# A macaron layer with two levels of seven-product matmuls: sums of weights kept in DRAM, and a down projection that accumulates in PSUM

## The chip, the core and the metric

The kernel runs on one core of a Trainium2 chip. The metric is the device time of one execution in microseconds (us); the figure for the kernel before is the median of three runs. A profile is one execution of the same program with the hardware profiler on. Engines are named as the profile names them: PE is TensorE (PEld its weight loads), DVE is VectorE, ACT is ScalarE, POOL is GpSimd, SP is SyncE, whose queue issues all DMAs here.

## What is computed

A layer of 2048 tokens by 512 features in float32: half of an MLP, then causal attention with 16 heads of 32, then half of the same MLP again. All three work on a layer norm of `x` and add to `x`.

```python
x = x + 0.5 * ffn(layernorm(x), gate, up, down)      # 4-bit codes and scales, 4096 rows
x = x + attn(layernorm(x), w_qkv, b_qkv, w_out, b_out)
x = x + 0.5 * ffn(layernorm(x), gate, up, down)      # the same weights

def ffn(x, Wg, Wu, Wd):                              # the weights are dequantized first
    g, u = x @ Wg.T, x @ Wu.T                        # 512 -> 4096
    return (gelu_tanh(g) * u) @ Wd.T                 # 4096 -> 512
```

## The kernel before

**Seven products for eight.** Each big matmul is split into 2 by 2 blocks and done as seven block products in place of eight (Winograd's form of Strassen's scheme). It needs sums of blocks of the weights (`s3 = a11 - a21`, `s2 = a22 - s3`, `a21 + a22`, `s4 = a12 - s2`), like sums of the tokens (`t3`, `t2`, `t1`, `t4`), and sums of the seven results.

**First MLP** (`ffn`, lines 186 to 570; its phase 2 isn't used). The 4096 rows are eight groups `g` of 512, each with two halves `h`. The codes are dequantized on DVE (`dequant_steps`, L217), the outer sums of the weights are made on POOL (`Rows.steps`, L263), and dequantized weights with their sums are written to DRAM (`keep`, L244) for the second MLP: 14 blocks of 128 by 256 for each `(g, h)`, and 14 for the down weights of each `g`. The order is written out by hand. `slot` (L320) does the seven gate and seven up products of one half for half of the tokens. After every product it runs `pump(rate)` (L309), which takes `rate` steps from the list `background` (the dequantizing and summing of coming weights, 20 steps for a half of a group, 16 for the down weights), and, in two of the four slots of a group, one token or down step of `sums` and one piece of the down projection (`down_pieces`, L386). At the end of a slot what is left in `background` is run at once. Codes are loaded when `Rows.load` or `down_steps` is called, that is before the steps that use them, in the SP queue.

**Attention** (`attention`, L1008) follows. In its pairs of heads 5 and 6 (L1383) it starts what the second MLP needs first: `load_first` fetches the weights of two pairs of problems, `sums_first` forms their inner sums. At its end (L1434 to L1444) come the last value products, eight pieces of the output projection, the last four divisions (reciprocals on DVE, L1253; multiplications on POOL, L1256) and four last pieces of the projection.

**Second MLP** (`second_ffn`, L599). Here the seven-product scheme is used twice, one level inside the other, and the tokens are done in two halves of 1024. An outer product `i` of `(g, h)` is called a problem; `problems` (L573) lists the 112 of one half of the tokens, seven to each `(g, h)`, in the order 1, 2, 6, 7, 5, 4, 3, and two neighbours form a pair: NP = 56 pairs for a half, numbered `n` = 0 to 111 through both. Seven pairs are one group `g`. In what follows "place" is `n % 7`.

- `fetch` (L583) loads a pair's weights into one of four ring slots, four pairs ahead. One DMA for each of the two problems brings the 4 blocks; `weight_sums` (L591) forms the inner sums in place, four POOL instructions for a pair, two pairs ahead of use.
- `pair` (L681) runs the seven inner products `y`. Each is four PE matmuls of 128x128 on 128x256. Products 1, 6, 7 and 4 add up in one PSUM bank `d`, 5 and 3 in a bank `f`, 2 has a bank `e`. The partial sums are read between them: after 1, 5 and 6 by ACT copies (L721, L726, L734), after 2, 7 and 3 by DVE additions (L730, L737, L740), after 4 by ACT (L743). So PE may issue 6 only after ACT has read 1, 7 after ACT has read 6, and 4 after DVE has read 7 (L737). Between them lie other products and, at "a" and "b" of the order (1, 5, 2, 6, a, 7, 3, b, 4), pieces of the down projection. Without pieces the order is (1, 5, 6, 2, 7, 3, 4). `hooks` are steps that are issued after the product of that count.
- `recombine` (L750) adds the results of the pair before (L758: of the 14 additions in a group, 10 on DVE and 4 on POOL, 1024 elements each), then gelu on ACT (L761) and the gating product on DVE (L770). The additions are issued at hook 1, gelus at hook 4, gating at hook 6.
- `down` (L800) does the down projection of a group during the seven pairs of the next group. `down_sums` are four DVE additions of 1024 elements (L809 to L812), all issued at place 1. Its 14 pieces (seven products for each of two quarters `q`) are run two to a pair. A piece is eight PE matmuls (L823) into a bank of its own, which DVE (L832) or ACT (L846) reads; sums of the seven results are made in SBUF by six DVE instructions, two ACT copies and five POOL additions (L838) for each `q`.
- `Tokens.outer` and `Tokens.inner` (L643, L658) form the sums of the tokens, on DVE but for one. They are issued at hooks of the first pairs of each half (L927 to L959); `Later` (L878) normalizes and transposes the second half of the tokens about pairs 53 to 56.
- PSUM has a pool `ps_one` of seven banks and `ps_acc` of one, which the second MLP before leaves unused.

Of the kernel before, what the change touches and what calls it, by code (L numbers as in the profile page):

```python
# [35 lines left out]
def macaron_kernel(ctx: ExitStack, tc: tile.TileContext, x, packed, scales, wqk, bqk, wv, bv, wo, bo, out):  # L36
# [147 lines left out]
    kept = {}  # L184

    def ffn(phase, finish, behind, loads, ready=(), first_w=None):
# [8 lines left out]
        with tc.tile_pool(name=f"w{phase}", bufs=1) as wp, tc.tile_pool(name=f"dq{phase}", bufs=1) as dq, tc.tile_pool(  # L195
# [52 lines left out]
            class Rows:  # L248
# [28 lines left out]
                def keep(self):  # L277
                    keep((self.g, self.h), self.flat)

# [243 lines left out]
            for g in range(NG):  # L523
# [13 lines left out]
                if phase == 1:  # L537
                    background += down_steps(wd, g)
                    second.keep()
                else:  # L540
                    nc.sync.dma_start(out=wd, in_=kept[g])
# [14 lines left out]
                if phase == 1:  # L556
                    keep(g, wd)
# [25 lines left out]
    def fetch(slot, pair):  # L583
        for k, (g, h, i) in enumerate(pair):
            place = {1: 0, 5: 1, 2: 2, 4: 3, 7: 4, 6: 5, 3: 6}[i]
            nc.sync.dma_start(
                out=slot[:, k, 0:4, :].rearrange("p (m c) n -> p m (c n)", m=2),
                in_=kept[g, h].rearrange("p (m i c n) -> p i m (c n)", m=2, i=7, c=2)[:, place],
            )

    def weight_sums(slot):  # L591
        a11, a12, a21, a22, s3, s2, s4 = [slot[:, :, y, :] for y in range(7)]
        eng = nc.gpsimd
        eng.tensor_tensor(s3, a11, a21, ALU.subtract)
        eng.tensor_tensor(s2, a22, s3, ALU.subtract)
        eng.tensor_tensor(a21, a21, a22, ALU.add)
        eng.tensor_tensor(s4, a12, s2, ALU.subtract)

    def second_ffn(finish, ready, slots):  # L599
# [9 lines left out]
        with tc.tile_pool(name="w2", bufs=1) as wp, tc.tile_pool(name="act2", bufs=1) as ap:  # L609
# [20 lines left out]
            class Tokens:  # L630


                def __init__(self, half, b1, b2):
                    nm = f"f2_{half}"
                    self.b1, self.b2 = b1, b2
                    self.ts, self.t4 = x_transposed(nm, 2), x_transposed(nm, 3)
                    self.ys = wp.tile([P, 7, 3, 256], F32, tag="ys", name=f"ys_{nm}")
# [5 lines left out]
                def outer(self, first):  # L643
                    b11, b21, b12, b22, t3, t2, t4 = [self.operand(x) for x in range(7)]
                    return [
                        lambda: first.tensor_tensor(t3, b22, b12, ALU.subtract),
                        lambda: tt(t2, t3, b11, ALU.add),
                        lambda: tt(b12, b12, b11, ALU.subtract),
                        lambda: tt(t4, b21, t2, ALU.subtract),
                    ]  # L650

                def first_sum(self, x):

                    if x < 2:
                        return self.t4[:, 2, 256 * x : 256 * x + 256]
                    return self.operand(x)[:, 0, 256:]

                def inner(self, t):  # L658
# [6 lines left out]
                    t1 = b12 if t > 0 else self.t4[:, 2, :].rearrange("p (x n) -> p x n", x=2)  # L665
                    return [
                        lambda: tt(t3, b22, b12, ALU.subtract),
                        lambda: tt(t1, b12, b11, ALU.subtract),  # L668
# [4 lines left out]
                def factors(self, i):  # L673
                    x = (None, 0, 1, 3, 6, 2, 5, 4)[i]
                    v = self.operand(x)
                    t3, t2, t4 = [self.ys[:, x, k, :] for k in range(3)]
                    return [None, v[:, 0, :256], v[:, 1, :256], v[:, 1, 256:], t4, self.first_sum(x), t2, t3]
# [3 lines left out]
            def pair(n, tokens, pieces, hooks):  # L681
# [3 lines left out]
                fa = [[None] + [a[:, k, y, :] for y in (0, 1, 6, 3, 2, 5, 4)] for k in range(2)]  # L685
# [16 lines left out]
                def product(ps, y, first=False):  # L702

                    for k in range(2):
# [3 lines left out]
                        )  # L708

# [89 lines left out]

            def down(half, g):  # L800


                def block(h, second):
# [5 lines left out]
                    lambda: tt(s3, block(0, 0), block(0, 1), ALU.subtract),  # L809
                    lambda: tt(block(0, 1), block(0, 1), block(1, 1), ALU.add),  # L810
                    lambda: tt(s2, block(0, 1), block(0, 0), ALU.subtract),
                    lambda: tt(s4, block(1, 0), s2, ALU.subtract),  # L812
                ]
                u = {}
                x_half = residual[:]

# [740 lines left out]
```

## Time and profile before

| what | value |
|---|---|
| median of three runs | 3265.59 us (3264.62 to 3267.82) |
| the profiled execution, its own time | 3266.22 us |
| its span, first to last instruction | 3264.4 us |
| granted PE clock, mean | 0.992 |
| PE, PEld, DVE, ACT, POOL busy in the span | 97%, 61%, 67%, 32%, 52% |
| first MLP, 0 to 1194 us: PE, DVE, POOL busy | 1178, 761, 616 us |
| attention, 1194 to 2107.57 us: PE, DVE, POOL busy | 901, 536, 233 us |
| second MLP, 2107.57 to 3264.4 us: PE, DVE, POOL busy | 1096, 904, 851 us |

A row of the view of stages has a window in us from the span's start, its length, the busy time of each engine in it with its number of instructions, the granted PE clock, the share of the DMA engines' time and GB/s. Matmuls overlap in the record: one of 128x256 is shown with 0.38 us, but four of them start 0.86 us after the four before (2306.87, 2307.73, 2308.59 us in the timeline), so that a busy PE isn't yet a PE at its pace. In the view of waits a line has who waited for whom, the total in us, how often, and the longest.

### The profile page before, as it was taken

How to read it: one execution, taken by the hardware profiler on the slowest of the kernel's cores; microseconds unless marked ns; L12 is line 12 of the kernel's file. 1: busy time of each engine (PE TensorE's matmuls, PEld its weight loads, DVE VectorE, ACT ScalarE, POOL GpSimd, SP SyncE). 2: the span in 40 equal slices, each digit the busy share in tenths (PEclk: the TensorE clock that was granted, in tenths of full speed). 3: DMA queues.
4: the chain of work that ended last, by engine and by line, in shares of the span. 5: the costliest groups of instructions: out<-in, count | busy, mean ns of one | idle time of the engine just before them, and what ended most of it. 6: DMA issues, size and time to landing. Idle time of an engine off the chain costs nothing.

```text
span 3264.4 us, 39140 instructions
## 1 busy us (share of the span) xinstructions
PE 3175.8 (97%) x14000; PEld 1987.7 (61%) x14000; DVE 2201.7 (67%) x3078; ACT 1044.7 (32%) x2134; POOL 1700.0 (52%) x1785
## 2 busy tenths in 40 slices
PE   8999999999999999999999999899999999999998
PEld 4556565655656565333344333378888878888887
DVE  6666666666666555575654665578778887777786
ACT  4111111111111131464543545433333333333332
POOL 3546364555546340332212233367778767777775
PEclk9999999999999999999999999999999999999999
DMA  4111111111111100000000000122222233222221
GB/s 142 65 71 42 65 71 49 65 65 71 42 65 65 52 17 7 6 15 6 13 4 6 21 19 8 67 90 84 78 81 84 75 104 126 75 75 84 78 81 56
DMA packets 118562, 186.91 MB, mean 57 GB/s; under 512 B 11176, under 2 KB 89000, under 8 KB 114400
## 3 DMA queue, kind: packets, MB, share of 16 engines
q1 hardware_dynamic: 118368, 184.41, 17.2%
q8 instruction: 111, 1.82, 0.2%
q14 instruction: 83, 0.68, 0.1%
HBM read 132.24 MB, written 50.56 MB: 56 GB/s over the span
## 4 chain that ended last, share of the span: by engine, by line
PE 84%; DVE 9%; issue 3%; ACT 2%; POOL 2%; DMA 0%; SPq 0%; DVEq 0%; POOLq 0%; ACTq 0%
PE po L414 12%; PE pu L315 11%; PE pg L315 11%; PE d_f L705 9%; PE po_f L823 9%; PE av L1217 8%; PE pm L1152 6%; PE f_f L705 4%; PE pqk L1063 4%; PE ps L1278 2%; PE e_f L705 2%; PE pv L1080 2%; PE pp L1102 1%; PE ps L1287 1%; DVE o_f L758 1%
## 5 line engine op out<-in xcount | busy, mean ns | idle before, releaser
L1167 DVE TENSOR_REDUCE parts<-pm 128x1 f32<-128x512 f32 (+3 forms) x640 | 370.5, 607 | 151.2 <-PE pm L1152 138.2
L705 PE MATMUL d_f<-ys_f,ring 128*128 128x256 f32 x1344 | 353.2, 386 | 48.8 <-DVE o_f L737 47.8
L1152 PE MATMUL pm<-kT,qT 32*128 32x512 f32 (+3 forms) x1280 | 335.6, 576 | 0.1
L1310 ACT ACTIVATE pt<-ps 128x512 f32<-128x512 f32 (+3 forms) x576 | 271.7, 532 | 131.7 <-PE ps L1287 130.8
L705 PEld LDWEIGHTS d_f<-ys_f,ring 128*128 128x128 f32 x1344 | 254.6, 192 | 95.8 <-DVE o_f L737 57.7
L1217 PE MATMUL av<-pt,vaug 128*64 128x512 f32 (+3 forms) x1280 | 301.2, 555 | 7.9 <-ACT both L1226 7.2
L1287 PE MATMUL ps<-qT,kT 32*128 32x512 f32 (+3 forms) x1280 | 279.0, 536 | 0.0
L758 DVE TENSOR_TENSOR o_f<-o_f,o_f 128x1024 f32<-128x1024 f32 x128 | 251.4, 1974 | 34.7 <-ACT o_f L743 32.5
L369 POOL TENSOR_TENSOR u<-u,u 128x512 f32<-128x512 f32 x64 | 81.9, 1279 | 345.2 <-ACT u L366 345.2
L1304 POOL TENSOR_SCALAR_AFFINE_SELECT pt<-pt 128x256 f32<-128x256 f32 x128 | 52.3, 408 | 396.4 <-ACT pt L1303 396.1
L823 PE MATMUL po_f<-wd_f,inter_f 128*128 128x256 f32 x1024 | 241.2, 379 | 1.6 <-DVE inter_f L770 1.6
L414 PEld LDWEIGHTS po<-wd,inter 128*128 128x128 f32 x1024 | 194.4, 190 | 77.5 <-issue 55.7
L414 PE MATMUL po<-wd,inter 128*128 128x256 f32 x1024 | 241.1, 379 | 0.0
L315 PE MATMUL pg<-xT_f,w 128*128 128x512 f32 x512 | 240.8, 598 | 0.0
L705 PE MATMUL f_f<-xT_f,ring 128*128 128x256 f32 x896 | 237.1, 388 | 3.6 <-DVE xT_f L668 3.6
L315 PE MATMUL pu<-xT_f,w 128*128 128x512 f32 x512 | 238.0, 592 | 0.0
L428 POOL TENSOR_TENSOR xq<-xq,d 128x512 f32<-128x512 f32 x124 | 160.3, 1303 | 114.3 <-DVE d L422 63.5
L823 PEld LDWEIGHTS po_f<-wd_f,inter_f 128*128 128x128 f32 x1024 | 194.4, 190 | 28.3 <-DVE inter_f L770 2.0
L705 PEld LDWEIGHTS f_f<-xT_f,ring 128*128 128x128 f32 x896 | 175.2, 196 | 29.6 <-DVE xT_f L668 2.5
L1217 PEld LDWEIGHTS av<-pt,vaug 128*64 128x64 f32 x1280 | 65.3, 135 | 209.3 <-issue 147.4
L823 PE MATMUL po_f<-wd_f,s_f 128*128 128x256 f32 x768 | 181.0, 379 | 1.3 <-issue 1.3
L414 PE MATMUL po<-wd,s 128*128 128x256 f32 x768 | 181.4, 379 | 0.0
(193 smaller groups left out, 6125.2 us busy)
## 6 DMA issues: line engine op xcount, KB each, us to landing
wd_f<-kept SPq DMA_DIRECT2D x112, 256.0 KB
kept<-wd SPq DMA_DIRECT2D x8, 1792.0 KB
xq<-in_x SPq DMA_DIRECT2D x16, 256.0 KB
pk<-in_gate_codes SPq DMA_DIRECT2D x16, 256.0 KB
sc<-in_gate_scales SPq DMA_DIRECT2D x32, 128.0 KB
pk<-in_up_codes SPq DMA_DIRECT2D x16, 256.0 KB
sc<-in_up_scales SPq DMA_DIRECT2D x32, 128.0 KB
pk<-in_down_codes SPq DMA_DIRECT2D x16, 256.0 KB
```

The lines of the kernel that those rows point to most:

```text
L315: nc.tensor.matmul(ps, lhsT=a[:, j, :], rhs=b[:, j, :], start=(j == 0), stop=(j == 1))
L414: nc.tensor.matmul(ps[:, j, :], lhsT=a[i][:, k, bass.ts(2 * q + j, P)], rhs=b[i][:, k, :], start=(k == 0), stop=(k == 1),)
L428: adder.tensor_tensor(dst, dst, other, ALU.add)
L705: nc.tensor.matmul(ps[:, k, :], lhsT=fa[k][y], rhs=fb[k][y], start=first and k == 0, stop=True, skip_group_check=True,)
L758: sums.append(lambda: eng.tensor_tensor(dst, dst, other, ALU.add))
L823: nc.tensor.matmul(ps[:, j, :], lhsT=a[:, k, bass.ts(2 * q + j, P)], rhs=wd[:, PLACE[i], k, :], start=(k == 0), stop=(k == 1),)
L1063: nc.tensor.matmul(ps, lhsT=w[:, j, k, :], rhs=xT[tb][:, k, :], start=(k == 0), stop=(k == 3))
L1152: nc.tensor.matmul(ps[a][:, :n], lhsT=q[r, bass.ts(4 * g + i, P)], rhs=k[r, kb * 512 : kb * 512 + n], start=True, stop=not on_pe,)
L1167: nc.vector.tensor_reduce(parts[:, a, i, kb : kb + 1], ps[a][:, :n], AX.X, ALU.max)
L1217: nc.tensor.matmul(av[64 * a : 64 * a + 64, off:], lhsT=vaug[:, c, p % 4, HD * a : HD * a + 2 * HD], rhs=pt[:, a, off:], start=(c == 0), s ...
L1287: nc.tensor.matmul(ps[a][:, off:], lhsT=k[r, bass.ts(c, P)], rhs=q[r, g * 512 + off : (g + 1) * 512], start=False, stop=True,)
L1310: nc.scalar.activation(pt[:, a, plain:], ps[a][:, plain:], AF.Exp, scale=scale)
```

## The change

Three things in the second MLP change, and the first MLP does more.

- **Inner sums of the weights.** The first MLP makes the four inner sums of all seven blocks (`inner_sums`) on POOL, in two parts of four and three blocks, into tiles of the tag `xn` (two buffers), and writes each part to DRAM (`kept_sums`): eight POOL instructions and eight DMAs for each `(g, h)`. They are steps of `background`. `fetch` now brings seven blocks in three DMAs for a problem, and `weight_sums` is gone.
- **Down projection.** Products 1, 6, 7 and 4 of a quarter add up in one bank (`ps_acc`; for the last quarter of all `ps_one`), 5 and 3 in another, 2 in a third, as the inner products do. ACT reads after 1, 6 and 5, DVE after 2, 7, 4 and 3: four DVE, three ACT and three POOL instructions for each `q`. The order is (1, 2, 6, 7, 4, 5, 3), named `DOWN`, for the first quarter and (1, 2, 6, 7, 5, 4, 3) for the second. The four `down_sums` are issued at places 1 (two), 2 and 3, and 1, 1, 2, 2, 2, 2 and 4 pieces at places 0 to 6. In the second half of the tokens pair 56 takes one piece and runs one after it, pair 57 takes none.
- **Sums of the tokens.** Those that the second MLP needs first are made at the end of attention on DVE (`outer_sums`, `inner_first`), ahead of the last value products and the last divisions. For the second half of the tokens two of the four outer sums go to POOL.

```diff
+                def inner_sums(self):
+                    key = self.g, self.h
+                    kept_sums[key] = store.tile([P, 4, 7, P], F32, tag=f"kept_sums_{key}", name=f"kept_sums_{key}")
+                    steps = []
+                    for part in (slice(0, 4), slice(4, 7)):
+                        a11, a12, a21, a22 = [self.w[:, m, part, c, :] for m in range(2) for c in range(2)]
+                        made = []
+                        def make(k, x, y, op, part=part, made=made):
+                            t = normed(f"inner_{phase}_{self.g}_{self.h}_{k}_{part.start}")
+                            t = t[:, : (part.stop - part.start) * P].rearrange("p (i n) -> p i n", n=P)
+                            made.append(t)
+                            nc.gpsimd.tensor_tensor(t, x, made[k - 1] if y is None else y, op)
+                            nc.sync.dma_start(out=kept_sums[key][:, k, part, :], in_=t)
+                        steps += [
+                            lambda f=make, x=a11, y=a21: f(0, x, y, ALU.subtract),
+                            lambda f=make, x=a22: f(1, x, None, ALU.subtract),
+                            lambda f=make, x=a12: f(2, x, None, ALU.subtract),
+                            lambda f=make, x=a21, y=a22: f(3, x, y, ALU.add),
+                        ]
+                    return steps
...
-                    background += down_steps(wd, g)
+                    background += down_steps(wd, g) + rows.inner_sums()
...
+                    background += second.inner_sums()
                     keep(g, wd)
...
-            nc.sync.dma_start(
-                out=slot[:, k, 0:4, :].rearrange("p (m c) n -> p m (c n)", m=2),
-                in_=kept[g, h].rearrange("p (m i c n) -> p i m (c n)", m=2, i=7, c=2)[:, place],
-            )
+            w = kept[g, h].rearrange("p (m i c n) -> p i m c n", m=2, i=7, c=2)[:, place]
+            nc.sync.dma_start(out=slot[:, k, 0:2, :], in_=w[:, 0])
+            nc.sync.dma_start(out=slot[:, k, 2, :], in_=w[:, 1, 1])
+            nc.sync.dma_start(out=slot[:, k, 3:7, :], in_=kept_sums[g, h][:, :, place, :])
...
-                if n + 2 < 2 * NP:
-                    mine[3].append(call(weight_sums, slot(n + 2)))
...
+    def outer_sums(b1, b2, ts, t4, eng):
+        b11, b21, b12, b22 = b1[:, 0:2, :], b1[:, 2:4, :], b2[:, 0:2, :], b2[:, 2:4, :]
+        s3, s2, s4 = ts[:, 0:2, :], ts[:, 2:4, :], t4[:, 0:2, :]
+        return [
+            lambda: eng.tensor_tensor(s3, b22, b12, ALU.subtract),
+            lambda: nc.vector.tensor_tensor(s2, s3, b11, ALU.add),
+            lambda: nc.vector.tensor_tensor(s4, b21, s2, ALU.subtract),
+            lambda: eng.tensor_tensor(b12, b12, b11, ALU.subtract),
+        ]
+    def inner_first(b1, t4):
+        v = b1.rearrange("p (x c) n -> p x c n", c=2)
+        t1, t3 = [t4[:, k, :].rearrange("p (x n) -> p x n", x=2) for k in (2, 3)]
+        return [
+            lambda: nc.vector.tensor_tensor(t3, v[:, :, 1, 256:], v[:, :, 0, 256:], ALU.subtract),
+            lambda: nc.vector.tensor_tensor(t1, v[:, :, 0, 256:], v[:, :, 0, :256], ALU.subtract),
+        ]
...
+                    key = "d" if i in (1, 6, 7, 4) else "f" if i in (5, 3) else "e"
+                    new = i in (1, 2, 5)
+                    if new:
+                        pool, tag = (ps_acc, "acc") if key == "d" and (q == 0 or not final) else (ps_one, "one")
+                        banks[key] = pool.tile([P, 2, 256], F32, tag=tag, name=f"po{key}_{nm}")
...
+                    if i in (1, 6, 5):
+                        u[i] = ap.tile([P, 2, 256], F32, tag=f"d{i}", name=f"d{i}_{nm}", bufs=1)
+                        nc.scalar.mul(u[i], ps, 0.5)
+                    if i == 2:
+                        from_bank(x11)
+                        add(x11, u[1])
...
+                    elif i == 7:
+                        from_bank(x22)
...
                     elif i == 4:
+                        from_bank(x21)
...
                     elif i == 5:
+                        add(x22, u[5])
...
+                    elif i == 3:
+                        from_bank(x12)
+                        add(x12, u[6])
...
+                orders = [(1, 2, 6, 5, 7, 3, 4)] * 2 if final else [DOWN, (1, 2, 6, 7, 5, 4, 3)]
+                return sums, [lambda i=i, q=q: piece(i, q) for q in range(2) for i in orders[q]]
...
-            at(0, 0, 0, *first[2:])
-            at(0, 0, 1, t2, t4)
-            at(0, 0, 2, *third[:2])
-            at(0, 0, 3, *third[2:])
-            at(0, 0, 4, t1)
-            at(0, 0, 6, *second[:1])
-            at(0, 1, 0, *second[1:])
-            at(0, 1, 2, *fourth)
+            for f in first[2:]:
+                f()
+            at(0, 0, 0, *third[:2])
+            at(0, 0, 1, *third[2:])
+            at(0, 0, 3, *second[:2])
+            at(0, 0, 5, *second[2:])
+            at(0, 1, 1, *fourth)
...
+            t3, t2, t4, t1 = outer_sums(*ready, nc.gpsimd)
             at(0, 55, 5, *first[:2])
             at(0, 55, 6, *first[2:])
-            at(1, 0, 6, t3, t2, t4, *third)
-            at(1, 1, 0, t1)
-            at(1, 1, 2, *second)
+            at(1, 0, 6, t3, t2, t4, *third[:3])
+            at(1, 1, 0, third[3])
+            at(1, 1, 1, t1)
+            at(1, 1, 3, *second)
             at(1, 1, 5, *fourth)
...
+                    for k, f in enumerate(down_sums):
+                        if due == (1, 1, 2, 3)[k]:
+                            mine[(2, 5, 2, 2)[k]].append(f)
+                    take = 0 if n == NP + 1 else (1, 1, 2, 2, 2, 2, 4)[due]
+                    mid = (take + 1) // 2
+                    plan = [pieces[:mid], pieces[mid:take]]
+                    del pieces[:take]
+                pair(n, tokens, plan if any(plan) else None, mine)
...
-                if p in (5, 6):
-                    next_w[p - 5]()
+                if p == 5:
+                    next_w()
...
             assert not later
+            xT_f += [x_transposed("f2_sums", tb) for tb in (2, 3)]
+            for step in outer_sums(*xT_f, nc.vector) + inner_first(xT_f[0], xT_f[3]):
+                step()
             while pending:
                 pending.pop(0)()
```

After the last pair the order changes too: one piece runs ahead of the last additions, gelus and gating products (before: two), the first two `down_sums` come next, then the second piece, the other two sums and the remaining twelve pieces.

## The prediction

> **What bounds the kernel now.** I read the page first, then the view of stages. PE is busy 97% of the span, and the other engines 67% at most.
>
> ```profile
> PE 3175.8 (97%) x14000; PEld 1987.7 (61%) x14000; DVE 2201.7 (67%) x3078; ACT 1044.7 (32%) x2134; POOL 1700.0 (52%) x1785
> ```
>
> The change removes no matmul, so it can only win back time in which PE waits or runs slowly. An undisturbed product of four 128x256 matmuls takes 0.862 us (starts at 2306.87, 2307.73, 2308.59), a pair with two pieces 11 of these, 9.49 us. The stages of the second MLP are its start (7 pairs), its steady part (47 and 52 pairs), the passage between the halves of the tokens (5 pairs) and its end:
>
> ```profile
> 2107.57:2166.34 58.77, 49.15 (x197) 38.04 (x196) 46.39 (x56) 20.08 (x33) 35.99 (x31) 0.94 0.43 143
> 2166.34:2639.22 472.88, 455.16 (x2069) 396.91 (x2068) 374.65 (x388) 158.20 (x270) 361.47 (x286) 0.99 0.28 83
> 2639.22:2702.76 63.54, 55.34 (x253) 47.10 (x252) 54.15 (x61) 25.80 (x44) 37.32 (x26) 0.95 0.33 104
> 2702.76:3222.14 519.38, 502.49 (x2290) 438.79 (x2289) 401.99 (x407) 174.54 (x298) 398.93 (x312) 0.99 0.28 84
> 3222.14:3264.40 42.26, 34.34 (x157) 29.28 (x155) 27.26 (x34) 6.88 (x12) 17.25 (x11) 0.99 0.21 69
> ```
>
> Lost against that pace: start 58.8 - 7 x 7 x 0.862 = 16.5 us; steady 472.9 - 47 x 9.49 = 26.9 and 519.4 - 52 x 9.49 = 25.9, together 53; passage 63.5 - 55 products (47.4) - 32 transposes (0.12 each, 3.8) = 12.3; end 42.3 - 39 x 0.862 = 8.6. That is 90 us, the most there is to win. The first MLP has PE full from 70 us on.
>
> Where do the 53 us lie? Four neighbouring pairs, places 0 to 3:
>
> ```profile
> 2377.80:2387.29 9.49, 9.49 (x45) 8.36 (x44) 8.61 (x9) 5.10 (x9) 9.41 (x7) 1.00 0.30 86
> 2387.29:2399.59 12.30, 9.77 (x45) 8.28 (x44) 12.27 (x12) 2.98 (x5) 7.21 (x6) 1.00 0.29 85
> 2399.59:2410.78 11.19, 11.19 (x46) 9.55 (x45) 6.30 (x8) 2.35 (x4) 6.72 (x6) 0.85 0.16 47
> 2410.78:2420.27 9.49, 9.49 (x45) 8.36 (x44) 7.55 (x7) 4.20 (x7) 7.00 (x5) 1.00 0.27 85
> ```
>
> At place 1 DVE has no idle time (12.27 of 12.30) and PE loses 2.8 us; at place 2 PE has a granted clock of 0.85 and loses 1.7 more. The view of waits of the second MLP names the releaser, and the timeline shows why it is late:
>
> ```profile
> PEld d_f L705 <- DVE o_f L737: 57.7, 26, 4.7
> PE d_f L705 <- DVE o_f L737: 47.8, 19, 4.3
> ```
>
> ```profile
> 2389.29 1.75 DVE L809 TENSOR_TENSOR s_f<-inter_f,inter_f 128x1024 f32<-128x1024 f32 x1
> ...
> 2390.96 1.75 DVE L758 TENSOR_TENSOR o_f<-o_f 128x1024 f32<-128x1024 f32 x1
> ...
> 2392.63 1.75 DVE L810 TENSOR_TENSOR inter_f<-inter_f,inter_f 128x1024 f32<-128x1024 f32 x1
> ...
> 2396.15 1.23 DVE L812 TENSOR_TENSOR s_f<-inter_f,s_f 128x1024 f32<-128x1024 f32 x1
> ...
> 2397.89 0.68 DVE L737 TENSOR_TENSOR o_f<-d_f,u_f 128x512 f32<-128x512 f32 x1
> ...
> 2398.62 1.13 PE L705 MATMUL d_f<-ys_f,ring 128*128 128x256 f32 x4 [2.54 <-DVE o_f L737]
> ```
>
> Product 4 waits for L737, which stands behind four `down_sums`. Those that run beside POOL's L594 to L597 take 1.75 us, the last one 1.23.
>
> **Steady part.** Three things ease L737.
>
> The POOL sums go: 110 x (1.25 + 1.10 + 1.00 + 0.93) = 471 us of 1157 in this stage. DVE's 1024-wide L758 (1.97 us in the mean, 160 of them) should near the undisturbed 1.23, L770 (1.02, 128 of them) the 0.68 that it also shows. Down pieces drop from 12 DVE instructions of 0.69 a group to 8, and from 10 POOL additions (1.3 to 1.6) to 6. DVE's work in a group falls from 10 x 1.97 + 8 x 1.02 + 21 x 0.68 + 12 x 0.69 + 5.7 (`down_sums`) = 56 us of about 70 to 12.3 + 5.4 + 14.3 + 5.5 + 4.9 = 42. And of the four sums only one stays ahead of L737 at place 1.
>
> I lay place 1 out anew: some 1.7 us of gating left over, one addition 1.2, L730 0.7, one sum 1.2, one piece 0.7, so DVE is free by 6.1; product 7 ends about 6.3 (1, 5, 2, 6, a piece of 1.72, 7). L737 isn't late. What is new is the cover: places 0 and 1 have one piece, at "a", so between 7 and 4 lies product 3 alone, 0.86 us against L737's 0.68 with its hand-overs. A pair without any piece shows what three such tight steps cost: 2153.20 to 2159.77, 6.57 against 6.03, so 0.54. I take 0.3 for each of two places: 14 groups x 0.6 = 8 us. Best 0.2 a group (3 us), worst 1.5 (21 us), if L758 stays at 1.97 beside what POOL keeps.
>
> The clock: [...] eight of the fourteen groups have such a stretch of 3.4 us at half clock, some 14 us in all, and the gain would be 31. The row decides: 0.85 follows a gap of 2.54. I count the slow stretch as going too. Steady gain 53 - 8 = **45 us** (31 to 50).
>
> PE's own new waits: a down piece that adds to a bank must wait for the ACT or DVE read before it. 1 to 6 and 6 to 7 are ACT copies (0.60 in L846), 7 to 4 a DVE read (0.69), 5 to 3 an ACT copy. In the plan of places at least two products (1.72 us) lie between each, so zero; without that cover 0.15 to 0.5 each, eight a group.
>
> Queues. A `fetch` is six DMAs of 896 KB in place of two of 512 KB: SP spends 0.57 us on each, 3.4 us a pair, and SP is not short of time. At the 338 GB/s seen in 2108 to 2124 us, 896 KB need 2.7 us of 9.5, and they are issued four pairs ahead. Zero; at the start they queue behind 2 MB of `away`: slot 2 lands by my sum at 2121, needed at 2126; a miss costs up to 4 us.
>
> **Start.** Six sums move to the end of attention. DVE idles there (2091.5 to 2098.1), but they wait for the last transposed tile (2095.8) and need 4 x 1.23 + 2 x 0.68 = 6.3 us, until 2102.1. Behind them stand four projection reads (2.5 us) and the reciprocals, which began at 2101.3 and now begin at 2104.6; POOL's multiplications and PE's last pieces wait for these: +3.2. Then pair 0 no longer waits for 2.05 us (L668) and 3.85 us (L737 behind eight sums), and pairs 1 to 3 (4.2, 2.1, 2.2 lost) shrink to about 0.7 each, since POOL is quiet. 3.2 - 5 - 6 + 2 (a half-clock stretch after the longer gap at the end of attention) = **-5** (-9 to +2).
>
> **Passage.** Outer sum t3 goes to POOL (2.36 against 1.23), +1.1; pair 57 has no cover by pieces, but less on DVE. I get 11 us lost for 12.3: **-1** (-5 to +4).
>
> **End.** One piece of 1.72 us fewer covers the last gating, and piece 6 waits for two sums (1.9 us); the last x12 addition (0.7) falls away, a slow stretch may come: **+2.5** (0 to +5).
>
> **First MLP.** 128 POOL instructions: 64 of 512 elements (1.27), 64 of 384 (about 1.0 between 0.73 and 1.27), 145 us, up to 190 beside DVE; POOL goes from 616 to about 780 of 1194. [...] by the rows, L339 takes 0.69 alone and 1.13 to 1.45 beside POOL, so 0.5 x 128 = 64. [...] More telling is the queue: two `xn` tiles mean that every second sum waits for a DMA (about 3 us, my estimate between SP's 0.53 for an issue and the 4.9 from issue to use of `xl`, 2661.17 to 2666.09), so the eight take some 17 us where their `pump` calls give 14. And the next codes (`Rows.load`) stand behind these DMAs in SP. Now they are issued 38 us ahead (551.36 for 589.14); after the change DVE's first dequantizing step of a half waits about 9 us. Behind it wait the reads of PSUM banks, but a product with its piece takes 3.44 us and two banks, two of every seven readers are ACT, and so the seven banks last PE some 16 us. So zero to 8: **+1**.
>
> Sum: -45 - 5 - 1 + 2.5 + 1 = -47.5 on the profiled execution's 3266.2; I take -46 for what I have missed. The median is 0.6 below the profiled run: **3220**.
>
> **Rivals.**
> - *One wait for another* (18%): tight steps between 7 and 4 with DVE still slow, 2 us a group instead of 0.6: gain 45 - 20 = 25, in all 3240. For it: L758 stays beside POOL additions at places 6 and 0. Against: POOL falls from some 55 to 19 us a group.
> - *More than I count* (12%): places 0 and 1 at 0.2 a group, start -9, passage -5: 3205.
> - *The codes come late* (5%, slower): each sum waits 4 us for its landing, eight take 32 us, 18 too late, with the load 23 after the slot's end. Each of 15 halves then costs PE 23 - 16 = 7 us, 105 in all: 3325. It turns the whole into a loss from 19 us of lateness on (15 x 3 = 46).
> - *DVE isn't relieved* (3%): L737 is as late as before, 3265.
> - The forecast itself 62%.
>
> What a measurement can tell from no change is about 0.2%, 6.5 us. The range 3207 to 3243 takes in the forecast's own bounds (start, passage and end don't all go one way) and the first rival. Faster 0.92, same 0.03, slower 0.05.
>
> **What would show it.** Steady pairs of 9.5 us at PEclk 1.00 and L737 gone from the top of the waits; L758 on DVE about 1.3 us; pairs at places 0 and 1 near 8.0 us (nine products, 7.76, and 0.3). In the first MLP 48.5 us for a slot with pieces, as now; if it grows, the codes are late. If pairs of a place with one piece last over 9 us, the first rival holds. If the last projection pieces don't shift by 3 us, my start is wrong.

## The result, and the profile after

The changed kernel takes 3217.99 us in the median of four runs (3215.76 to 3220.36), against 3266.70 of the kernel before in runs beside it: a ratio of 0.9852 (95% interval 0.9835 to 0.9869). 3220 was predicted, in 3207 to 3243. The profiled execution took 3218.9, its span 3217.1, so 47.3 less than before; the sum came to 47.5. That is nearer than its terms deserve: two of them missed by 7 and 8 us, in opposite directions; 2.2 us won and 2.2 us lost are chances of the slow clock (below, "Start"); and the largest term, right in size, adds up three reliefs of which either of two would nearly have done alone.

The same views as before, first the page:

```profile
PE 3168.7 (98%) x14000; PEld 1978.9 (62%) x14000; DVE 2073.8 (64%) x3011; ACT 1059.2 (33%) x2166; POOL 1300.8 (40%) x1404
```

The stages of the second MLP (start, steady, passage, steady, end; the columns are those of the prediction's fence, with the granted clock, the share of DMA and GB/s last):

```profile
2104.27:2153.35 49.08, 46.06 (x198) 35.50 (x197) 36.15 (x49) 19.97 (x33) 10.47 (x4) 1.00 0.74 231
2153.35:2600.51 447.16, 446.78 (x2054) 388.56 (x2053) 313.37 (x360) 163.92 (x283) 122.91 (x69) 1.00 0.43 127
2600.51:2670.02 69.51, 58.44 (x254) 49.61 (x252) 45.32 (x54) 26.10 (x45) 18.58 (x9) 0.90 0.40 121
2670.02:3167.45 497.43, 497.43 (x2289) 433.56 (x2288) 338.16 (x380) 181.28 (x313) 137.82 (x74) 1.00 0.43 128
3167.45:3217.10 49.65, 41.90 (x173) 35.09 (x171) 23.19 (x27) 8.98 (x15) 11.91 (x7) 0.88 0.22 69
```

PE is as good as full in the steady stages; passage and end are longer than before (69.5 for 63.5, 49.7 for 42.3; the end now holds four more products, 3.4 us, as fewer pieces run in earlier pairs). The stages start 3.3 us earlier, at 2104.27. Places 0 to 2, the same group as before:

```profile
2354.99:2363.01 8.02, 8.02 (x37) 6.75 (x36) 6.32 (x8) 4.50 (x8) 1.27 (x1) 1.00 0.56 167
2363.01:2371.04 8.03, 8.03 (x37) 6.76 (x36) 6.84 (x10) 2.88 (x5) 1.27 (x1) 1.00 0.39 114
2371.04:2380.54 9.50, 9.50 (x46) 8.36 (x45) 7.91 (x8) 2.95 (x5) 2.36 (x1) 1.00 0.32 97
```

At place 1 POOL works 1.27 us where it worked 7.21, and DVE 6.84 of 8.03, where it had no idle time. At place 2 the clock is 1.00, where it was 0.85. The timeline of place 1 has the addition, the one sum that is left ahead, and the instruction that product 4 waits for (L770, formerly L737):

```profile
2364.51 1.21 DVE L791 TENSOR_TENSOR o_f<-o_f 128x1024 f32<-128x1024 f32 x1
...
2366.48 1.22 DVE L845 TENSOR_TENSOR s_f<-inter_f,inter_f 128x1024 f32<-128x1024 f32 x1
...
2369.33 0.69 DVE L770 TENSOR_TENSOR o_f<-d_f,u_f 128x512 f32<-128x512 f32 x1 [0.24 <-PE d_f L737]
...
2370.07 1.13 PE L737 MATMUL d_f<-ys_f,ring 128*128 128x256 f32 x4
```

L770 now waits for PE, not for DVE's queue; it starts 6.3 us after the start of its pair, where it had been 10.6.

### The profile page after: what moved, and what is told of

The parts are those of the page before. It is cut to its first block, busy times and chain, and to the rows that moved or that the text cites. A ratio compares the mean times of both kernels' runs of the same rounds, so it can differ in the third digit from the quotient of the medians.

```text
span 3217.1 us, 39429 instructions
## 1 busy us (share of the span) xinstructions
PE 3168.7 (98%) x14000; PEld 1978.9 (62%) x14000; DVE 2073.8 (64%) x3011; ACT 1059.2 (33%) x2166; POOL 1300.8 (40%) x1404
## 4 chain that ended last, share of the span: by engine, by line
PE 93%; DVE 2%; ACT 2%; issue 1%; POOL 1%; DMA 0%; SPq 0%; POOLq 0%; DVEq 0%; ACTq 0%
PE d_f L737 12%; PE po L438 12%; PE pu L339 12%; PE pg L339 11%; PE av L1250 8%; PE pod_f L866 7%; PE f_f L737 6%; PE pm L1185 6%; PE pqk L1096 4%; PE pof_f L866 3%; PE e_f L737 3%; PE ps L1311 2%; PE pv L1113 2%; PE poe_f L866 2%; PE pp L1135 2%; PE ps L1320 2%
## 5 line engine op out<-in xcount | busy, mean ns | idle before, releaser
L737 PE MATMUL d_f<-ys_f,ring 128*128 128x256 f32 x1216 | 321.4, 385 | 7.1 <-DVE o_f L770 7.0
L737 PEld LDWEIGHTS d_f<-ys_f,ring 128*128 128x128 f32 x1216 | 228.3, 191 | 54.7 <-DVE o_f L770 21.7
L791 DVE TENSOR_TENSOR o_f<-o_f,o_f 128x1024 f32<-128x1024 f32 x128 | 203.6, 1601 | 57.5 <-ACT o_f L776 53.7
L791 POOL TENSOR_TENSOR o_f<-o_f,o_f 128x1024 f32<-128x1024 f32 x48 | 128.7, 2682 | 142.7 <-ACT o_f L776 141.5
L881 POOL TENSOR_TENSOR xq<-xq,d_f 128x512 f32<-128x512 f32 x48 | 64.8, 1350 | 293.5 <-DVE xq L875 228.1
L438 PEld LDWEIGHTS po<-wd,s 128*128 128x128 f32 x768 | 145.5, 190 | 57.9 <-issue 39.9
L339 PE MATMUL pg<-xsum,w 128*128 128x512 f32 x384 | 177.8, 592 | 0.0
L339 PE MATMUL pu<-xsum,w 128*128 128x512 f32 x384 | 177.7, 592 | 0.0
L881 POOL TENSOR_TENSOR xq_second<-xq_second,d_f 128x512 f32<-128x512 f32 x45 | 61.5, 1366 | 272.9 <-DVE xq_second L875 217.6
```

The lines of the kernel that those rows point to most:

```text
L339: nc.tensor.matmul(ps, lhsT=a[:, j, :], rhs=b[:, j, :], start=(j == 0), stop=(j == 1))
L438: nc.tensor.matmul(ps[:, j, :], lhsT=a[i][:, k, bass.ts(2 * q + j, P)], rhs=b[i][:, k, :], start=(k == 0), stop=(k == 1),)
L737: nc.tensor.matmul(ps[:, k, :], lhsT=fa[k][y], rhs=fb[k][y], start=first and k == 0, stop=True, skip_group_check=True,)
L791: sums.append(lambda: eng.tensor_tensor(dst, dst, other, ALU.add))
```

## The experiments

Time lost against PE's pace, by stage, in the profiled execution of each kernel (products and transposes counted as in the prediction; "end" up to the last product, us). In the column of pair 0, differences of up to 3 us come from the first 72 us of the execution, where the slow clock varies from run to run:

| kernel | median, us | ratio to before (95%) | pair 0 at | start | steady | passage | end |
|---|---|---|---|---|---|---|---|
| before | 3266.70 | | 2107.6 | 16.5 | 53.5 | 12.3 | 3.5 |
| changed | 3217.99 | 0.9852 (0.9835–0.9869) | 2104.3 | 6.8 | 9.3 | 18.3 | 8.7 |
| e_spread | 3219.77 | 0.9862 (0.9849–0.9876) | 2106.9 | 16.6 | 8.5 | 11.0 | 3.5 |
| e_kept | 3205.07 | 0.9814 (0.9801–0.9828) | 2098.6 | 11.9 | 2.9 | 14.6 | 3.5 |
| e_down | 3241.14 | 0.9926 (0.9913–0.9938) | 2106.9 | 17.6 | 22.0 | 15.3 | 7.7 |
| e_pool_idle | 3272.26 | 1.0016 (1.0010–1.0023) | 2099.6 | 14.8 | 63.1 | 15.2 | 3.5 |
| e_sums_later | 3258.30 | 0.9979 (0.9970–0.9987) | 2100.1 | 17.6 | 53.3 | 12.6 | 3.5 |
| e_fetch_late | 3213.46 | 0.9835 (0.9822–0.9849) | 2103.8 | 6.8 | 11.0 | 15.2 | 7.9 |
| e_outer_dve | 3214.48 | 0.9838 (0.9824–0.9851) | 2105.1 | 6.8 | 9.7 | 12.6 | 8.1 |
| e_outer_late | 3221.90 | 0.9861 (0.9848–0.9875) | 2107.4 | 8.1 | 9.8 | 19.8 | 7.9 |
| e_end | 3213.29 | 0.9834 (0.9821–0.9847) | 2103.4 | 6.8 | 9.3 | 17.9 | 4.5 |
| e_best | 3198.70 | 0.9792 (0.9779–0.9805) | 2102.0 | 10.7 | 2.1 | 8.3 | 3.5 |
| e_best_down | 3211.65 | 0.9831 (0.9818–0.9845) | 2098.2 | 10.7 | 9.7 | 12.4 | 8.3 |

Two causes for the late L737 were to be told apart: the four sums that stand ahead of it in DVE's queue (theory Q in what follows), and POOL's sums, beside which each DVE sum takes longer (theory C). My theory after the result was S: kept sums and spread sums each ease L737 enough by themselves.

**One part alone.** First only the order of the four `down_sums` in the kernel before:

```
-                if due == 1 and pieces:
+                if pieces:
                     for k, f in enumerate(down_sums):
-                        (mine[k] if n != NP + 1 else mine[6]).append(f)
+                        if due == (1, 1, 2, 3)[k]:
+                            mine[(2, 5, 2, 2)[k] if n != NP + 1 else 6].append(f)
```

> The kernel before, with its four down_sums spread over pairs as the change spreads them (the first at place 1 after step 2, the block sum at place 1 after step 5, the third at place 2, the fourth at place 3); weight_sums on POOL, the down pieces and everything else as before. Theory Q (L737 was late because four sums stood ahead of it in DVE's queue): the stall at place 1 and the slow stretch behind it go, of the 53 us lost in steady pairs about 15 stay, the time is near 3228. Theory C (it was late because POOL's sums made every DVE instruction slow): DVE has as much to do as before, L758 stays at 1.97 us, the loss is only shared out over places 1 to 3, at most 15 us are won, 3251. Theory S (the two are substitutes, each alone is enough): near 3228 here, and the run with kept sums alone is near 3225 as well.

3219.8: three changed lines give as much as the whole change. Place 1:

```profile
2376.98:2386.48 9.50, 9.50 (x46) 8.36 (x44) 9.16 (x11) 2.88 (x5) 7.23 (x6) 1.00 0.27 83
```

POOL works 7.23 us there, as before (7.21), L758 still takes 1.99 us in the mean, and yet 45 of the 53 us are gone. Theory C as the only cause falls: it is enough to take sums out of L737's way.

Then only the kept sums (`inner_sums`, the new `fetch`, no `weight_sums`), with the four `down_sums` in a row as before:

> The kernel before, with the inner sums of weights kept by the first MLP and fetched, and no weight_sums on POOL; down pieces, down_sums and token sums as before. Four sums ahead of L737 at place 1 at 1.23 in place of 1.75 us, and L758 likewise, make it 2.1 of its 2.54 us earlier. Theory C: nearly all of the 53 us of steady pairs goes, with 8 in attention (no POOL sums ahead of the mask there) and 5 at the start: near 3205 to 3212. Theory S: some 10 us stay at place 1 and with the earlier end of the gap the slow stretch goes: 3266 - 43 - 8 - 5 + 1 = about 3212 to 3225. Theory Q: four sums are still ahead, the loss at place 1 falls from 2.95 to some 2 us and the slow stretch stays in half the groups: steady -20, attention -8, 3238.

3205.1, the figure of theory C and lower than the whole change. The timeline of place 1:

```profile
2361.73 1.22 DVE L826 TENSOR_TENSOR s_f<-inter_f,inter_f 128x1024 f32<-128x1024 f32 x1
2362.87 1.22 DVE L775 TENSOR_TENSOR o_f<-o_f 128x1024 f32<-128x1024 f32 x1
2364.00 1.22 DVE L827 TENSOR_TENSOR inter_f<-inter_f,inter_f 128x1024 f32<-128x1024 f32 x1
2365.14 0.69 DVE L747 TENSOR_TENSOR o_f<-e_f,u_f 128x512 f32<-128x512 f32 x1
2365.74 1.22 DVE L828 TENSOR_TENSOR s_f<-inter_f,inter_f 128x1024 f32<-128x1024 f32 x1
2366.99 1.23 DVE L829 TENSOR_TENSOR s_f<-inter_f,s_f 128x1024 f32<-128x1024 f32 x1
...
2368.73 0.68 DVE L754 TENSOR_TENSOR o_f<-d_f,u_f 128x512 f32<-128x512 f32 x1
```

The queue ahead of L754 (L737 before) is as long as ever, but each of its 1024-wide instructions takes 1.22 or 1.23 and none 1.75, and it starts 7.0 us after the pair (2361.71). PE loses 0.02 us at such a place. So S holds in its claim that each alone ends nearly all of the loss, and together they can't win it twice; its figure for this run (3212 to 3225) was too high, since it let 10 us stay at place 1.

Last the down part alone (accumulation in PSUM, the plan of pieces, spread sums, the new end):

> The kernel before, with the down product accumulated in PSUM, its pieces and sums spread over pairs, and the new order at the end; weight_sums on POOL stay. Theory Q or S: steady pairs win about 40 of the 53 us, the end loses 4, 3230. Theory C: POOL's sums still stretch DVE's instructions (L758 at 1.7 us or more); 20 us are won, 3246. The attention, the start and the passage between the halves of the tokens are as before within 2 us.

3241.1, between the two forecasts, and by 21 us slower than `e_spread`, which has the same spread sums. Places 0 and 1 of the group:

```profile
2373.02:2381.10 8.08, 8.04 (x37) 6.76 (x36) 7.22 (x8) 4.50 (x8) 7.74 (x7) 1.00 0.36 100
2381.10:2389.31 8.21, 8.04 (x38) 6.76 (x36) 8.21 (x10) 2.97 (x5) 4.44 (x4) 1.00 0.24 65
```

With one piece 7.76 us would be due; in the mean of the groups 0.40 and 0.57 are lost at these two places, together 13.6 us, where `e_spread` loses 0.03 and 0.02; this is what `e_down` loses more in the steady pairs (13.5). They are the tight steps of the prediction, dearer here than the 0.27 of the changed kernel, with POOL's sums beside them. The rest is passage (+4.3 against `e_spread`) and end (+4.2). Accumulation and the plan of pieces were not run apart; that the loss lies at the two places with one piece points to the plan.

**Is it POOL's load?** Kept sums, and POOL's four sums a pair again, into a tile that nobody reads:

```
+        eng.tensor_tensor(t, a11, a21, ALU.subtract)
+        eng.tensor_tensor(t, a22, t, ALU.subtract)
+        eng.tensor_tensor(t, a21, a22, ALU.add)
+        eng.tensor_tensor(t, a12, t, ALU.subtract)
...
+                if n + 2 < 2 * NP:
+                    mine[3].append(call(idle_sums, slot(n + 2), idle))
```

> The kernel before with kept sums (the run that took 3205.07), to which POOL's four sums per pair are put back at their old place, but into a scratch tile that nothing reads; the products use the kept sums. Extra work for POOL only, no product waits for it. If the kept sums won the steady pairs by taking load off POOL (DVE's instructions beside it are shorter), the stall at place 1 comes back: about 45 to 52 us of steady loss, L758's counterpart near 1.97 us, 3250 to 3257. If they won because products had waited for weight_sums themselves: the time stays at 3205 to 3207.

3272.3: all that the kept sums had won in the steady pairs is lost again. No engine waits for these POOL instructions, and the timeline of place 1 shows what they do:

```profile
2382.49 1.74 DVE L834 TENSOR_TENSOR s_f<-inter_f,inter_f 128x1024 f32<-128x1024 f32 x1
...
2383.23 1.59 POOL L621 TENSOR_TENSOR idle<-ring 128x256 f32<-128x256 f32 x1
2384.16 1.74 DVE L783 TENSOR_TENSOR o_f<-o_f 128x1024 f32<-128x1024 f32 x1
2384.89 1.59 POOL L622 TENSOR_TENSOR idle<-ring,idle 128x256 f32<-128x256 f32 x1
...
2385.82 1.75 DVE L835 TENSOR_TENSOR inter_f<-inter_f,inter_f 128x1024 f32<-128x1024 f32 x1
...
2388.09 1.21 DVE L836 TENSOR_TENSOR s_f<-inter_f,inter_f 128x1024 f32<-128x1024 f32 x1
...
2391.81 1.23 PE L730 MATMUL d_f<-ys_f,ring 128*128 128x256 f32 x4 [2.88 <-DVE o_f L762]
```

Until POOL ends, at 2386.48, DVE's sums take 1.74; behind it 1.21. Product 4 is late by 2.88. The ends of the lines: L621 ends at 2384.82 and L783 1.08 us later, at 2385.90; L622 ends 0.58 after that and L835 1.09 after L622. So each of these two DVE sums, which began beside a POOL instruction, ended 1.08 to 1.09 us after that one's end, little less than the 1.13 to 1.14 at which such sums follow each other undisturbed in `e_kept`. POOL's 128x256 sums take 1.59 us here, where the kernel before has 0.73 in attention (L594, below).

The loss is 10 us larger than before (63.1 for 53.5), more than I forecast. Half of it are three more slow stretches in the steady pairs (11 for 8, 1.7 us each), the other half gaps that are 0.35 us longer (2.86 for 2.51 in most groups), because DVE gets to the first sum 2.35 us after the start of the pair (2382.49 and 2380.14) instead of 2.00 (2389.29 and 2387.29 before). Why it does is open.

**Attention.** The changed kernel's first 8 us are won far from the change's target, in head pair 6 of attention. Before, `sums_first` stood in POOL's queue ahead of a causal mask (L1304), and exp on ACT, the copy behind it and PE waited:

```profile
1924.56 0.73 POOL L594 TENSOR_TENSOR ring<-ring 128x256 f32<-128x256 f32 x1
...
1930.27 0.41 POOL L1304 TENSOR_SCALAR_AFFINE_SELECT pt<-pt 128x256 f32<-128x256 f32 x1
1930.71 0.42 ACT L1312 ACTIVATE pt<-pt 128x256 f32<-128x256 f32 x1 [5.57 <-POOL pt L1304]
...
1932.89 1.97 PE L1217 MATMUL av<-pt,vaug 128*64 128x512 f32 x4 [5.46 <-ACT both L1226]
```

The eighth POOL sum ends at 1930.3, and only then the mask runs. The kernel before with these sums elsewhere (`extra = {14: [next_w[1]]}` at head pair 6):

> The kernel before, with sums_first (eight weight_sums on POOL for pairs 0 and 1) issued in the middle of head pair 6 of attention instead of at its start, so that they don't stand ahead of the diagonal's affine_select on POOL. Theory: the 5.5 us wait of PE at about 1930 us and the slow stretch behind it go, -8, 3258.5. Rival (the 8 us that the changed kernel wins there are a chance stretch of slow clock): no change within 1 us. A second rival: the sums in the middle hold up another mask, and the wait only moves.

3258.3, and pair 0 starts 7.5 us earlier, with the same slow stretches ahead of attention as before. So it is the place of these sums in POOL's queue, and not a chance of the clock.

**What the changed kernel gave back.** Four edits of it, in this order: fetches of pairs 53 to 55 at step 4 of the next pair; `outer_sums(*ready, nc.vector)`; the six token sums behind the divisions; in the last group (1,q0), (1,q1), the gating, (2,q0), (2,q1), then the rest.

> The changed kernel, with the fetches behind pairs 53, 54 and 55 issued at step 4 of the following pair, behind that pair's loads of xl, instead of ahead of them in SP's queue. Theory (in the passage between the halves, xl waits in SP's queue behind six DMAs of a fetch, normalize on ACT waits for it and u_f's copy behind normalize): the loss of pairs 54 to 58 falls from 18.3 to about 13 us, the time from 3218 to about 3213. Rival (t3 on POOL and DVE beside it are what made the passage longer): no change within 1.5 us.

3213.5. In the timeline of the changed kernel the loads of `xl` (L662) stand behind the six DMAs of a fetch in SP's queue, and the chain runs over ACT to PE:

```profile
2624.53 0.42 SPq L612 DMA_DIRECT2D ring<-kept_(0, 0)_271  x1
...
2628.62 1.04 SPq L662 DMA_DIRECT2D xl<-away  x2
...
2632.97 0.81 ACT L941 ACTIVATE xl<-xl,nbias,rstd 128x512 f32<-128x512 f32 x1 [3.82 <-DMA xl<-away]
2633.68 0.56 ACT L767 COPY u_f<-d_f 128x512 f32<-128x512 f32 x1
...
2634.30 1.13 PE L737 MATMUL d_f<-xT_f_sums,ring 128*128 128x256 f32 x4 [3.19 <-ACT u_f L767]
```

With the fetch behind the loads, pair 56 loses 3.5 us in place of 7.9. The passage loses 15.2 for 18.3 (13 was expected), since pairs 57 and 58 give 1.3 back. The medians differ by 4.5, but the intervals of the two ratios overlap; the stage is the surer witness.

> The changed kernel, with the outer sums of the second half of the tokens (t3, t1) on DVE instead of POOL. By the trace t3 takes 2.34 us on POOL and t1 3.33, and pair 57 waits 2.69 us at its start: if POOL's share of the passage is the larger one, the loss there falls by 3 to 4 us, 3214; if the transfer of xl sets it, by under 1.5, 3217.

3214.5; the passage loses 12.6 for 18.3. Pairs 57 and 58 lose 2.7 less, and this is t3 and t1. The other 3.0 lie in pair 56, at whose end t3 only begins; there a slow stretch is missing (6.8 us of half clock in the passage for 13.6), and this can be chance. In a kernel with both edits (`e_best`, below, which also has the down pieces of before) the passage loses 8.3.

> The changed kernel, with the six sums of tokens at the end of attention behind the last divisions in DVE's queue instead of ahead of them. Theory (they hold up the projection's reads and the reciprocals, and this is the 4 us by which the time from the last projection to pair 0 grew): the end of attention gets about 4 us shorter, pair 0 then waits for part of the 6.3 us of sums, together -1 to -3, 3215 to 3217. Rival (the sums are needed by pair 0 either way): no change or up to +3.

3221.9. My theory fell, and the timeline names what I had not thought of:

```profile
2095.91 7.78 POOL L1289 TENSOR_TENSOR attnT<-both,den 32x128 f32<-32x128 f32 x8 [15.23 <-DVE den L1286]
2098.03 1.16 DVE L621 TENSOR_TENSOR xT_f_sums<-xT_f 128x1024 f32<-128x1024 f32 x1
...
2104.76 4.86 DVE L1138 TENSOR_TENSOR xq<-pp,xq 128x512 f32<-128x512 f32 x8
2105.58 2.05 PE L1135 MATMUL pp<-wo_bo,attnT 128*128 128x512 f32 x2 [3.50 <-DVE xq L1138]
```

The sums now run beside POOL's eight multiplications, which take 7.78 us where they took 4.09, and the reads of the projection stand behind the sums. From the first of the last projection matmuls to pair 0: 10.6 us before, 14.7 after the change, 17.0 here (some 1.7 us of each of the last two are a slow stretch behind the gap).

> The changed kernel, with piece 1 of the second quarter and piece 2 of both quarters moved forward in the last group: (1,q0), (1,q1), then the last gating, (2,q0), (2,q1), then 6, 5, 7, 3, 4 of each quarter. Theory (the 3.9 us that the end lost came of one piece of 1.72 us less ahead of the last gating, and of a slow stretch of clock behind the gap): the gap of 3.26 us falls to 1.6, the 0.72 us wait for the second sum goes and the slow stretch with them, -4 to -6, 3213. Rival (the tail behind the last product decides): the pieces' end moves but the stores end at the same distance, -2 at most; a slow stretch that stays: -2.

3213.3, and the waits of the end agree. Changed kernel, then this one:

```profile
PE poe_f L866 <- DVE inter_f L803: 3.3, 1, 3.3
```

```profile
PE pof_f L866 <- DVE inter_f L847: 1.7, 1, 1.7
PE poe_f L866 <- DVE inter_f L803: 1.6, 1, 1.6
```

The gap behind the gating (L803) halves and no slow stretch follows; a new wait of 1.7 us for a sum of blocks (L847) appears. The end loses 4.5 for 8.7.

**Put together.** Kept sums, spread `down_sums`, the down pieces and end of before, the two repairs of the passage, and three token sums at the end of attention:

> A kernel put together from what the runs showed: kept sums; the down pieces, their order and the end as in the kernel before, its down_sums spread over places 1 to 3; three of the six token sums (t3 and the two of inner_first, 2.6 us) at the end of attention, where DVE is idle for 2.3 us, the rest at pair 0 and 1; the fetches of the passage behind the loads of xl; the outer sums of the second half on DVE. Theory: of 2.9 us in the steady pairs about 1 stays, passage 14.6 to about 10, start 11.9 to about 7 with at most 1 us of slip at the end of attention: 3205 - 2 - 4.5 - 4 = about 3195. Rival: the small stalls replace one another, and it takes 3202 to 3205.

3198.7, the fastest of all: 6.4 us under `e_kept`, though not the 10 forecast. The stages, start and passage with their neighbours:

```profile
2101.99:2154.91 52.92, 47.71 (x198) 36.76 (x197) 40.42 (x54) 19.97 (x33) 10.47 (x4) 0.97 0.70 222
2154.91:2601.92 447.01, 446.63 (x2069) 392.75 (x2068) 342.76 (x388) 156.11 (x270) 159.74 (x95) 1.00 0.44 129
2601.92:2661.51 59.59, 54.09 (x253) 46.08 (x252) 48.90 (x60) 25.77 (x44) 18.38 (x10) 0.97 0.46 142
```

Passage and steady part came as hoped; the start still loses 10.7 (7 expected), probably because three sums moved are not six. They slip nothing: from the last projection to pair 0 it takes 10.6 us again. Pair 0 is late by 3.4 against `e_kept` all the same: 2.2 of it are two slow stretches of the clock in attention, where PE does the same work in both kernels, and 0.9 lie in the first 72 us of the execution.

The same with the changed kernel's down part:

> The kernel of the run before (3198.7 us), but with the changed kernel's way of the down product: accumulated in PSUM, one piece at places 0 and 1, its own end. It tells what this part costs by itself once the kept sums are there. Theory (one piece at places 0 and 1 leaves product 4 the cover of one product only, 0.27 us lost at each of 28 such places; one piece less at the end; less cover in pairs 57 and 58): steady +6.5, end +4 with its shorter tail, passage +2, so 3211. Rival (the down part is free, and what the changed kernel loses against kept sums alone comes from the token sums and POOL's t3): 3198 to 3201. A second rival: it gains, as DVE's work falls by another 4%: under 3197.

3211.7 where 3211 was expected: 13 us slower than `e_best`. In the profiled executions it is 11.6: steady 9.7 for 2.1, passage 12.4 for 8.3, end 8.3 for 3.5, less 1.0 for its shorter tail and 3.8 for pair 0, which starts earlier because the two slow stretches in attention are missing here (2.2) and the first 72 us are shorter (1.4).

## Why the prediction was right, and where it was not

**Steady part: -44 measured, -45 predicted.** The stall's place and releaser, the slow clock behind it and the new cost of two tight steps (0.27 us each at places 0 and 1, 0.3 taken) are as told. Its weak step is "Three things ease L737", which books all three and doesn't ask what each gives alone. Taking POOL's sums away gives 51 us alone, spreading the sums 45 alone, and fewer DVE instructions in the down pieces nothing that a run shows. The down part, which I booked as a gain with 8 us of new cost, is a cost only, once the kept sums are there: 13 us by `e_best_down`. "DVE's L758 should near the undisturbed 1.23" is also wrong: it takes 1.60 in the mean (1.70 in `e_kept`), and DVE's work in a group falls from 55 to 46 us, not to 42. This is the mean over places; what counts is place 1, where POOL has one instruction left and the addition takes 1.21.

**The clock.** I let the slow stretches go with the gaps because the row showed 0.85 behind a gap of 2.54; the lower bound of 31 left them standing. Steady pairs of the changed kernel have no slow stretch, so the row was right; and in `e_pool_idle`, where the gaps are back (2.86 in most groups), ten of twelve are followed by one.

**Start: -13, not -5.** Of this 9.7 lie in pairs 0 to 6, somewhat less than told (-5 - 6). The end of attention is 4.1 us longer, a gap of 2.33 and the slow stretch behind it (1.7), where I had taken 3.2 and 2. But pair 0 starts 3.3 us earlier where these two would have put it 5.2 later. PE's instructions of the two kernels, matched one by one in their order, show the parts:

- -7.8 at the place of `sums_first` in attention. This is the missing term: I counted `weight_sums` per pair and forgot the eight of `sums_first`, a queue in which a removed step had stood.
- -2.2 in the first 72 us, where the kernel before has 6.8 us of half clock and the changed one none. The first new sum runs at 88 us, so this is luck.
- +2.2 from two slow stretches in attention, at 2024 and 2072 us, which other runs with the same gaps don't have (luck again), and +0.4 earlier in attention.
- +4.1 at attention's end.

**Passage: +6, not -1.** "SP is not short of time. Zero": true for the steady pairs, false here, where a load that is needed within one pair stands behind six issues instead of two. And +1.1 for t3 on POOL was too little: DVE's t2 waits 2.41 us for it, and beside t1 (3.33 us on POOL) a `down_sums` addition on DVE takes 3.37 us instead of 1.22; the instruction that product 4 waits for stands behind it (3.75 us, and 2.82 with t1 on DVE).

**End: +3.9, within 0 to 5.** The mechanism is as told; the slow stretch that "may come" came (10.2 us at half clock).

**First MLP: 0, within 0 to 8.** From 72 us on its length is as before; POOL works 774 us for about 780 told, and PE is full from 70 to 1070 us. POOL is idle ahead of the 128 sums for 27 us in all, so they wait less for their DMAs than I assumed. DVE's work grew by 15 us (761 to 776), not by 64. The 64 took each of the 128 new sums to cost DVE 0.5 us; those of 512 elements take 1.28 and 1.37 us in the mean, hardly more than the undisturbed 1.27, so few of them meet a DVE instruction that makes them longer.

**The rivals.** None of them took over. What the first one priced at 2 us a group, the two places with one piece, cost 0.54; and the codes did not come late.

So -44 - 13 + 6 + 3.9 + 0 = -47: the missed sums in attention (-8) paid for the passage, 7 us worse than told. That the sum meets the forecast within 0.2 us is luck.

## What to carry to other kernels

When several parts of a change ease one wait, run each alone: the gain comes once, and every part brings its costs; here three lines gave what the whole change gave, and leaving one of its parts out gave 13 us more (3212 to 3199, in `e_best_down` and `e_best`). Work on POOL that nobody waits for may still hold up DVE (1.74 us for a sum of 1.21 in `e_pool_idle`), so look at how long an instruction takes beside it and without, at the place that counts and not in the mean. A step that is moved or removed is to be counted in every queue it stood in and every queue it joins, also in stages that the change isn't about.

## What the runs showed of the hardware

- DVE's sums and POOL's instructions took longer beside each other. From pair 7 on in the kernel before, 159 DVE instructions of 128x1024 began beside a POOL instruction and took over 1.5 us, and all of them ended 1.08 to 1.09 us after it; so did all 60 in the changed kernel. Such a sum takes 1.22 us undisturbed, 1.75 beside POOL's sums of 128x256 and 3.37 beside a long one (t1 in the passage, 3.33 us on POOL). POOL's 128x256 sum takes 0.73 us in attention and 1.59 beside DVE's sums in `e_pool_idle`, its eight 32x128 multiplications 4.09 beside DVE's reciprocals and 7.78 beside its token sums (`e_outer_late`).
- DVE additions that read one operand from a PSUM bank took no longer beside POOL: L730, L737 and L740 of the kernel before take 0.67 to 0.69 us in all 112 cases each, and 264 of these 336 began beside a POOL instruction.
- Accumulating a down product in a bank that is read between its products cost PE nothing where two pieces or more cover it: 0.02 us lost in a pair at places 2, 4, 5 and 6 of the changed kernel and 0.06 at place 3, the same to 0.01 as in `e_best`, where every piece has a bank of its own.
- The length of a gap alone didn't tell whether the half clock followed. In steady pairs of the kernel before it followed 8 of 12 gaps (2.5 to 3.3 us), in `e_pool_idle` 10 of 12 (2.9 us, one 3.5); in the kernel before, gaps of 2.5 us are among both kinds. In the traces of the kernel before and of the changed one the slow stretches last 3.41, 6.83 or 10.24 us (but for the last in each, which the end cuts short), and in each trace they begin at whole multiples of 3.413 us from one another, to within 5 ns. I laid the second MLP of both out in steps of 3.413 us from there. In the step ahead of a slow stretch PE idled 1.96 to 3.41 us (17 cases), in the 627 steps at full clock that were followed by full clock 1.91 at most. That is what these two traces show, and not why. In attention the same line doesn't hold: in the changed kernel PE idled 1.46 and 1.89 us in the steps ahead of two slow stretches, in the kernel before 1.61 in one that full clock followed.
